# A graph-attention layer on one core: section ends combined in 13 blocks inside the loop, and a final stage whose value bias is added by TensorE

## The chip, the cores and the metric

The kernel runs on one core of a Trainium2 chip. The metric is the device time of one execution in microseconds (us). All times here are in us from the start of the profiled span unless they are marked otherwise. The engines are named as the profile names them: PE (TensorE), DVE (VectorE), ACT (ScalarE), POOL (GpSimd) and SP (SyncE, which here only issues DMAs).

## The reference

400,000 edges, sorted by target, join 12,500 nodes of 128 channels. What must be computed, cut to what matters here:

```python
h = relu(layernorm(x))
msg = (h @ w_src + b_src)[src] + (h @ w_dst)[dst]
msg = msg * edge_weight * radial_mlp(edge_attr)
msg = (msg @ w_sep + b_sep).reshape(E, 8, 32)
score = einsum(smooth_leaky_relu(msg[:, :, :16]), alpha_dot)     # E x 8 heads
att = segment_softmax(score, dst)                                # over each target's edges
out = segment_sum(msg[:, :, 16:] * att, dst)                     # 12500 x 128
return x + out @ w_proj + b_proj
```

## The kernel before

**Node stage** (lines 149 to 347). Two tables `t_src` and `t_dst` are made from x, four tiles of 128 nodes at a time (`quads`, 25 of them), and written to HBM. In passing, `cuts` (line 303, called at quad 20) prepares constants of the edge stage: DVE works out `far` and `tgt`, and PE multiplies the value bias by the projection (`v_out`). `ends_d` holds in HBM the first and the last target of every section.

**Edge loop** (`windows`, line 661). 500 edges make a section, two sections a step. `for k in range(-5, NP)` runs 400 full steps; the order of the instructions on each engine is that of the program text, since `tc.manual_schedule()` is in force. Step k loads, gathers, multiplies and scores the edges of pair k, and sums the weighted values of pair c = k - 13 (`LAG`), because a softmax over 16 sections (one every 8 steps, `MP`) lies between. `gather` (line 742) makes POOL issue an indirect DMA per 128 edges, 3125 in all. `sums` (line 933) adds the values of a section into a window of 64 target rows; ACT copies the sums out of PSUM (`ob`, three buffers). `store_win` writes them to `win`, and `store` writes 63 rows of each window to `agg`, whose address is read from `base`. Two windows can overlap in `agg`, so SP holds a store back until the store before it has landed. `softmax_up`, `softmax_down`, `softmax_exp` and `softmax_T` come at steps with k % 8 = 2, 3, 3 and 4. The PSUM tile `misc` has one buffer, and `mlp1`, `sums`, `softmax_T` and `prep_turn` share it.

**Tail of the loop** (line 1196). 16 more steps (400 to 415) have nothing to gather; they finish the values of the last 13 pairs. Between them stand the `jobs` that combine section ends: a target whose edges cross a section's end has partial sums in several windows, so first and last rows of all 800 sections (1600 ends) are rescaled and added along the list by scans on DVE. The jobs do this in wide pieces: ends, maxima and rows are loaded, then 1536 ends go through `maxima`, `factors`, `columns`, `totals`, `quotients` and `back` at once; the last 64 ends follow after the last step (line 1202). `scatter` (line 1173) writes 13 pieces of 128 combined rows to `agg` by indirect DMAs on POOL.

**Final stage** (line 1251), outside the branch and with a schedule of its own. ACT issues eight loads of x plus bias (`x_fin`, from `xb`); SP loads `agg` in groups of 12 tiles (`load_g`, four buffers). `quotients` (DVE) divides by the softmax sums, `turn` transposes four tiles on PE and copies them on ACT, `finish` multiplies by `w_proj` on PE. On DVE, `finish` then adds the value bias to x once per tile (line 1308) and the product to x once per four tiles (line 1312), and SP stores the result.

Of the kernel before, what the change touches and what calls it, by code (L numbers as in the profile page):

```python
# [30 lines left out]
P = 128  # L31
# [25 lines left out]
def gnn_kernel(ctx: ExitStack, tc: tile.TileContext, a: dict, out: bass.AP):  # L57
# [20 lines left out]
    win = dram.tile([NS * W, ROW], F32, name="win")  # L78
    ends_d = dram.tile([1, 2 * NS + 2], I32, name="ends_d")
# [69 lines left out]
    with tc.tile_pool(name="node", bufs=2) as np_, tc.tile_pool(name="node1", bufs=1) as n1, \  # L149
# [145 lines left out]

        w_score = const.tile([C, C], F32, name="w_score")
# [6 lines left out]
        def cuts():  # L303
# [357 lines left out]
    def windows():  # L661
# [5 lines left out]
        with tc.tile_pool(name="wk2", bufs=2) as sp, tc.tile_pool(name="ps", bufs=1, space=PSUM) as pp, \  # L667
                tc.manual_schedule(), ExitStack() as held:
            lp = held.enter_context(tc.tile_pool(name="ld", bufs=2))
# [277 lines left out]
            def store(c, f):  # L947
                at = nc.sync.value_load(base[0:1, f, c:c + 1])
                nc.sync.dma_start(out=agg[ds(at, W - 1), :], in_=accs[c][f * W:(f + 1) * W - 1, :])


            def load_x(i):
                xs[i] = lp.tile([P, 4, C], F32, name="xs")
# [11 lines left out]

            def has(k):
                return 0 <= k < NP
# [6 lines left out]
            def step(k):  # L974
                c = k - LAG
                if has(c - 2):
                    store_win(c - 2)
                    store(c - 2, 0)
# [11 lines left out]
                if has(c - 2):  # L990
                    store(c - 2, 1)
# [58 lines left out]
                if has(c - 1):  # L1050
                    sums(c - 1)
                if has(k + 1):
# [17 lines left out]
            cp = held.enter_context(tc.tile_pool(name="cm", bufs=1))  # L1070
            NE = 2 * NS
            NA = NE // (4 * P) * 4 * P
            NC = -(-NE // P)
            differ = cp.tile([P, NE + 1], BF16, name="differ")
            cuts = cp.tile([P, NE], BF16, name="cuts")
            mx = cp.tile([P, NE], F32, name="mx")
            up = cp.tile([P, NE + 1], F32, name="up")
            de = cp.tile([P, NE], F32, name="de")
            rn = cp.tile([P, NE], F32, name="rn")
            obs = cp.tile([P, NC, ROW], F32, name="obs")  # L1080
            ids = cp.tile([P, NC], I32, name="ids")
            rows_w = win.rearrange("(s w) c -> s w c", w=W)
            rrs, nodes, tots = {}, {}, {"n": rn}

            def ends_load():
                nodes[0] = cp.tile([P, NE + 2], I32, name="node")
                nc.sync.dma_start(out=nodes[0], in_=ends_d[0:1, :].to_broadcast([P, NE + 2]))
                nodes[1] = cp.tile([NC, 2, P], I32, name="to")
                nc.vector.memset(nodes[1], -1)
                for j in range(2):  # L1090
                    nc.sync.dma_start(out=nodes[1][0:NC - 1, j, :], in_=ends_d[:, 1 + j:1 + j + (NC - 1) * P]
                                      .rearrange("o (g p) -> (o g) p", p=P))
                    nc.sync.dma_start(out=nodes[1][NC - 1:NC, j, 0:NE - (NC - 1) * P],
                                      in_=ends_d[:, 1 + j + (NC - 1) * P:1 + j + NE])

            def maxima_load(e0, e1):
                at = max_d[0:1, e0:e0 + 1]
                nc.sync.dma_start(out=mx[:, e0:e1], in_=bass.AP(
                    at.tensor, at.offset, [[NE, H], [0, C // H], [1, e1 - e0]]))

            def rows_load(g):
                rrs[g] = cp.tile([P, 4, ROW], F32, name="rr", bufs=2)
                q = P // 2
                for i in range(2):
                    nc.sync.dma_start(
                        out=rrs[g][i * q:(i + 1) * q], in_=rows_w[g * 4 * q:(g + 1) * 4 * q, i * (W - 1), :]
                        .rearrange("(j p) c -> p j c", j=4))

            def marks():
                nc.vector.tensor_tensor(differ, nodes[0][:, 1:NE + 2], nodes[0][:, 0:NE + 1], op=ALU.not_equal)  # L1110
                nc.vector.tensor_scalar(cuts, differ[:, 0:NE], RESTART, None, op0=ALU.mult)
                nc.vector.memset(up[:, 0:1], 0.0)
                nc.gpsimd.memset(obs[:, :, C:ROW], 1.0)
                tots["d"] = cp.tile([P, NE], F32, name="node")

            def places():
                on = cp.tile([NC, P], F32, name="on")
                to = nodes[1]
                nc.vector.tensor_tensor(on, to[:, 0, :], to[:, 1, :], op=ALU.is_equal)
                nc.vector.scalar_tensor_tensor(on, on, SKIP, to[:, 0, :], op0=ALU.mult, op1=ALU.add)  # L1120
                pt = pp.tile([P, NC], F32, name="m1")
                nc.tensor.transpose(pt, on, ident[:NC, :NC])
                nc.vector.tensor_copy(ids, pt)

            def maxima(e0, e1):
                nc.vector.tensor_tensor_scan(up[:, 1 + e0:1 + e1], cuts[:, e0:e1], mx[:, e0:e1],
                                             up[:, e0:e0 + 1] if e0 else RESTART, op0=ALU.add, op1=ALU.max)

            def factors(e0, e1):

                e = slice(e0, e1)
                nc.vector.tensor_add(de[:, e], up[:, e0:e1], cuts[:, e])
                nc.vector.tensor_sub(de[:, e], de[:, e], up[:, 1 + e0:1 + e1])
                nc.scalar.activation(de[:, e], de[:, e], AF.Exp)
                nc.vector.tensor_sub(mx[:, e], mx[:, e], up[:, 1 + e0:1 + e1])
                nc.scalar.activation(mx[:, e], mx[:, e], AF.Exp)
                nc.vector.tensor_mul(mx[:, e0 + 1:e1:2], mx[:, e0 + 1:e1:2], differ[:, e0 + 1:e1:2])

            def columns(g):

                pt = pp.tile([P, 2, 4, P], F32, name="p3")
                rx = cp.tile([P, 4, C], F32, name="rx")
                nc.scalar.copy(rx.rearrange("p j (h k) -> p j h k", h=H),
                               rrs[g][:, :, C:ROW].unsqueeze(3).to_broadcast([P, 4, H, C // H]))
                for j in range(4):
                    nc.tensor.transpose(pt[:, 0, j, :], rrs[g][:, j, 0:C], ident)
                    nc.tensor.transpose(pt[:, 1, j, :], rx[:, j, :], ident)
                e = slice(g * 4 * P, (g + 1) * 4 * P)
                for k, r in enumerate(tots.values()):
                    nc.vector.tensor_mul(  # L1150
                        r[:, e].rearrange("p (j s i) -> p j i s", j=4, i=2),
                        pt[:, k].rearrange("p j (i s) -> p j i s", i=2),
                        mx[:, e].rearrange("p (j s i) -> p j i s", j=4, i=2))

            def totals(e0, e1):
                for r in tots.values():
                    nc.vector.tensor_tensor_scan(r[:, e0:e1], de[:, e0:e1], r[:, e0:e1],
                                                 r[:, e0 - 1:e0] if e0 else 0.0, op0=ALU.mult, op1=ALU.add)

            def quotients(e0, e1):  # L1160
                e = slice(e0, e1)
                nc.vector.tensor_scalar(de[:, e], tots["d"][:, e], 1e-16, None, op0=ALU.add)
                nc.vector.reciprocal(de[:, e], de[:, e])
                nc.vector.tensor_mul(mx[:, e], rn[:, e], de[:, e])

            def back(g0, g1):
                pt = pp.tile([P, 4, P], F32, name="pa")
                w = min(P, NE - (g1 - 1) * P)
                for g in range(g0, g1):
                    nc.tensor.transpose(pt[:w, g - g0, :], mx[:, g * P:g * P + w], ident)  # L1170
                nc.scalar.copy(obs[:w, g0:g1, 0:C], pt[:w, 0:g1 - g0, :])

            def scatter(g):
                w = min(P, NE - g * P)
# [189 lines left out]
```

## Time and profile before

| what | us |
|---|---|
| median of 3 runs (lowest, highest) | 4316.28 (4314.72, 4322.2) |
| the profiled execution's own time | 4315.26 |
| its span, first to last instruction | 4313.4 |
| node stage, until the first load of the loop | 0 to 111.2 |
| gathers, first start to last end | 118.4 to 4108 |
| last full step ends on PE | 4115.3 |
| last copy of window sums (L941) ends | 4205.4 |
| first load of `agg` in the final stage (L1268) | 4229.3 |
| end | 4313.4 |

The span is busy on PE for 94%, on DVE for 72%, on POOL for 70% and on ACT for 49%. The windows view puts busy times beside the granted clock of TensorE: 982.8 of 1000 us of PE from 1000 to 2000 at clock 1.00, and 10.4 of 25 us from 4175 to 4200 at clock 0.71. "Idle before" in a row of the timeline is what the engine spent before that instruction, with what ended it. SPq, ACTq and POOLq are the issuing of DMAs.

### The profile page before, as it was taken

The numbers are of one execution on the slowest core, as the hardware profiler recorded it, in microseconds if no ns is written. First come the engines' busy times: TensorE is split into PE (matmuls) and PEld (weight loads), VectorE is DVE, ScalarE is ACT, GpSimd is POOL, SyncE is SP. The second block draws the span as 40 slices with busy tenths as digits, with TensorE's granted clock in tenths as the row PEclk, the third lists the DMA queues.
The fourth block names the chain that finished last, engine by engine and source line by source line (L and its number), as shares of the span: only waits on it lengthen the run. The fifth ranks groups of instructions, "written<-read, shape, count | busy, mean of one in ns | idle before, by whom it ended". The sixth has DMA issues, their size and how long they took to land.

```text
span 4313.4 us, 91919 instructions
## 1 busy us (share of the span) xinstructions
PE 4065.7 (94%) x31567; PEld 2626.4 (61%) x31567; DVE 3101.8 (72%) x5980; ACT 2105.5 (49%) x4995; POOL 3037.4 (70%) x3148
## 2 busy tenths in 40 slices
PE   6679999999999999999999999999999999999974
PEld 5346666666666666666666666666666666666653
DVE  7357777777777777777777777777777777777776
ACT  6335555555455455455555455454555545544521
POOL 0667777777777777777777777777777777777701
PEclk8789999999999999999999999999999999999987
DMA  5667777777777777777777777777777767777725
GB/s 207 196 183 183 183 193 184 192 194 185 194 188 186 192 190 186 192 183 185 198 186 193 185 177 190 183 182 185 175 181 188 177 182 184 182 185 178 173 59 190
DMA packets 598603, 790.10 MB, mean 183 GB/s; under 512 B 125595, under 2 KB 475424, under 8 KB 597996
## 3 DMA queue, kind: packets, MB, share of 16 engines
q1 hardware_dynamic: 394314, 520.94, 43.1%
q0 software_dynamic: 100416, 205.45, 23.2%
q10 hardware_dynamic: 103394, 57.74, 5.1%
q8 instruction: 250, 4.10, 0.4%
q14 instruction: 229, 1.88, 0.1%
HBM read 643.48 MB, written 140.67 MB: 182 GB/s over the span
## 4 chain that ended last, share of the span: by engine, by line
PE 80%; DMA 8%; ACT 3%; DVE 3%; issue 2%; POOL 2%; SPq 1%; ACTq 0%; POOLq 0%; DVEq 0%
PE V L926 16%; PE pa L840 14%; PE misc L937 9%; PE pm L829 6%; PE p L800 6%; PE pm L819 6%; PE p L783 5%; PE m L768 5%; PE m L854 4%; PE pm L822 4%; DMA gs<-t_src,idx 4%; POOL gs L749 2%; PE m L759 2%; ACT L842 1%; DMA agg<-z 1%
## 5 line engine op out<-in xcount | busy, mean ns | idle before, releaser
L749 POOL DMA_INDIRECT gs<-t_src,idx x3125 | 3023.0, 967 | 1082.9 <-issue 778.6
L842 ACT ACTIVATE sl<-pa,c_b_a 128x500 f32<-128x500 f32 x800 | 541.8, 677 | 1004.4 <-PE pa L840 996.8
L926 PEld LDWEIGHTS V<-c_w_v,mT 128*125 128x125 f32 x6192 | 735.3, 188 | 479.8 <-DVE ohT L793 231.9
L928 DVE TENSOR_TENSOR pvx<-V,Pem 125x512 f32<-125x512 f32 x774 | 530.9, 686 | 524.2 <-PE V L926 495.5
L926 PE MATMUL V<-c_w_v,mT 128*125 128x128 f32 x6192 | 875.3, 285 | 0.2 <-DVE pvx L928 0.2
L840 PE MATMUL pa<-mT,c_w_a 128*128 128x500 f32 x1600 | 817.4, 593 | 53.8 <-DVE al L847 51.8
L847 DVE SCALAR_TENSOR_TENSOR al<-pa,sl 128x500 f32<-128x500 f32 x800 | 542.3, 678 | 239.6 <-ACT sl L842 227.0
L822 PEld LDWEIGHTS pm<-ident,gs 128*128 128x128 f32 x2350 | 418.6, 192 | 380.0 <-issue 359.5
L807 DVE SCALAR_TENSOR_TENSOR rad<-p,c_fc_b,w_b 128x500 f32<-128x500 f32 x800 | 553.3, 733 | 104.2 <-PE p L800 101.4
L835 DVE SCALAR_TENSOR_TENSOR mT<-pm,c_b_src,rad 128x500 f32<-128x500 f32 x800 | 553.2, 733 | 79.9 <-PE pm L829 66.1
L937 PE MATMUL misc<-pvx,oh 125*64 125x136 f32 x6400 | 463.7, 288 | 0.0
L937 PEld LDWEIGHTS misc<-pvx,oh 125*64 125x64 f32 x6400 | 361.1, 138 | 163.7 <-ACT eT L761 157.3
L819 PE MATMUL pm<-ident,gs 128*128 128x128 f32 (+9 forms) x2725 | 436.9, 275 | 13.1 <-DMA gs<-t_src,idx 12.7
L800 PE MATMUL p<-h,w3b 64*128 64x500 f32 x1600 | 406.5, 585 | 11.1 <-ACT h L786 11.1
L786 ACT ACTIVATE h<-p,b 128x500 f32<-128x500 f32 x400 | 326.3, 816 | 177.1 <-PE p L783 134.5
L941 ACT COPY ob<-misc 128x136 f32<-128x136 f32 x400 | 108.9, 272 | 618.3 <-PE misc L937 533.7
L822 PE MATMUL pm<-ident,gs 128*128 128x12 f32 (+30 forms) x2350 | 384.2, 244 | 16.5 <-DMA gs<-t_src,idx 15.7
L819 PEld LDWEIGHTS pm<-ident,gs 128*128 128x128 f32 (+9 forms) x2725 | 339.2, 157 | 30.2 <-DMA gs<-t_src,idx 18.3
L829 PE MATMUL pm<-ohT,m 64*128 64x500 bf16 x2400 | 325.6, 378 | 0.0
L840 PEld LDWEIGHTS pa<-mT,c_w_a 128*128 128x128 f32 x1600 | 243.1, 192 | 81.4 <-DVE al L847 65.6
L768 PE MATMUL m<-eT,w1b 64*128 64x250 f32 x800 | 276.7, 426 | 7.5 <-ACT Sp L857 6.5
L768 PE MATMUL misc<-eT,w1b 64*128 64x250 f32 x800 | 276.7, 426 | 0.0
(151 smaller groups left out, 4227.0 us busy)
## 6 DMA issues: line engine op xcount, KB each, us to landing
w_b<-in_edge_weight SPq DMA_DIRECT2D x400, 500.0 KB
d_b<-in_dst SPq DMA_DIRECT2D x400, 250.0 KB
e_t<-in_edge_attr ACTq DMA_DIRECT2D x400, 125.0 KB
gs<-t_src,idx POOLq DMA_INDIRECT x3125
sc_d<-Sp SPq DMA_DIRECT2D x200, 250.0 KB
win<-ob SPq DMA_DIRECT2D x400, 68.0 KB
agg<-ob SPq DMA_DIRECT2D x800, 33.5 KB
md<-t_dst SPq DMA_DIRECT2D x800, 32.0 KB
```

The lines of the kernel that those rows point to most:

```text
L749: nc.gpsimd.indirect_dma_start(out=gs[:, t - t0, :], out_offset=None, in_=t_src[:, :], in_offset=bass.IndirectOffsetOnAxis(ap=idx[:, t:t + ...
L768: nc.tensor.matmul(p1[q], w1b[s, :], eTs[k][s, :], start=True, stop=True)
L800: nc.tensor.matmul(p3s[k][:, f, 0:SEC], w3b[s, :], h2s[k][s, :], start=True, stop=True)
L807: nc.vector.scalar_tensor_tensor(rad[:, s], p3[:, f, 0:SEC], b3, w_g[k][:, s], op0=ALU.add, op1=ALU.mult)
L819: nc.tensor.matmul(pms[k, f][:, a - e0:b - e0], gath[k // 16, t][:n], ident[:n, :n], start=(a == e0), stop=False, is_transpose=True, skip_ ...
L822: nc.tensor.matmul(pms[k, f][:, a - e0:b - e0], gath[k // 16, t], ident[:, a - t * P:n], start=(a == e0), stop=False, skip_group_check=True)
L829: nc.tensor.matmul(pms[k, f], m3[k][s, j, :], ohT[k][s, :], start=False, stop=(j == 2), skip_group_check=True)
L835: nc.vector.scalar_tensor_tensor(mTs[k][:, s], pms.pop((k, f)), b_n, rad[:, s], op0=ALU.add, op1=ALU.mult)
L840: nc.tensor.matmul(pa, w_a, mTs[k][:, f * SEC:(f + 1) * SEC], start=True, stop=True)
L842: nc.scalar.activation(sl, pa, AF.Silu, bias=b_a, scale=1.0)
L926: nc.tensor.matmul(V[:, t, :], mTs[c][:, o:o + T], w_v, start=True, stop=True)
L937: nc.tensor.matmul(acc[f * W:(f + 1) * W, :], ohs[c][:, f * TS + t, :], pvx[c][:, f, t, :], start=(t == 0), stop=(t == TS - 1), skip_group ...
```

## The change

The section ends are no longer combined in wide pieces in the tail. They are cut into 13 blocks of 128 ends (64 sections, 32 steps; the last has 64 ends). Blocks 0 to 10 are combined wholly inside the full steps of the loop, at fixed steps: load at k % 32 = 15, `block_maxima` at 17, `block_factors` at 19, `block_columns` at 20, `block_totals` at 21, `block_out` at 23. Block 11 falls on steps 399 to 407, and block 12 follows the last step. Ends are no longer divided; undivided sums with their weights are kept, and the final stage divides every row. Blocks 0 to 10 are parked in HBM (`obs_d`), and loaded and scattered one per step from step 400 on. `places`, which works out the scatter's row numbers, moves into `cuts` of the node stage. The tail has 14 steps (to 413); in these the window of `sums` is stored in the same step and not two steps later. The last stores and the scatters are declared free of each other.

The final stage moves into the same branch and schedule. Its x is loaded by ACT in the steps from 404 on, one load a step; all groups of `agg` have buffers of their own and are loaded at once; and the value bias is added by TensorE: `turn_has` transposes the 12 columns `has` of a group, and each tile's product gets a second matmul of `hasT` with `vsel`, in which row t of block t holds `v_out`. The pool `ld` moves to the other side of the memory, and `xs` has one buffer instead of two.

```diff
+            places()                        # at the end of cuts(), node stage
-                if has(c - 2):
+                if has(c - 2) and k <= NP:      # so too for store(c - 2, 1)
                     store_win(c - 2)
                     store(c - 2, 0)
...
                 if has(c - 1):
                     sums(c - 1)
+                    if k >= NP:
+                        store_win(c - 1)
+                        store(c - 1, 0)
+                        store(c - 1, 1)
...
+                for j in (k - LATE) // SB, (k - LATE) // SB - 1:     # SB = 32, LATE = 47
+                    o = k - LATE - j * SB
+                    if 0 <= j < NC - 1 and o in stages:
+                        stages[o](j)
...
+            def block_factors(g):
+                w, up, mx = width(g), ups[g], mxs[g][:, 0:width(g)]
+                de = des[g] = sp.tile([P, P], F32, name="de", bufs=1)[:, 0:w]
+                nc.vector.tensor_add(de, up[:, 0:w], cuts.pop(g)[:, 0:w])
+                nc.vector.tensor_sub(de, de, up[:, 1:1 + w])
+                nc.vector.tensor_sub(mx, mx, up[:, 1:1 + w])
+                nc.scalar.activation(de, de, AF.Exp)
+                nc.scalar.activation(mx, mx, AF.Exp)
+                nc.vector.tensor_mul(mx[:, 1:w:2], mx[:, 1:w:2], differ.pop(g)[:, 1:w:2])
+            def block_columns(g):
+                w, rr = width(g), rrs.pop(g)
+                rx = sp.tile([P, C], F32, name="rx", bufs=1)
+                nc.scalar.copy(...)                              # 8 weights spread over 128 columns
+                pt = small()                                     # the PSUM tile misc
+                nc.tensor.transpose(pt[:, 0, 0:w], rr[:w, 0:C], ident[:w, :w])
+                nc.tensor.transpose(pt[:, 1, 0:w], rx[:w, :], ident[:w, :w])
+                ...                                              # two products on DVE
+            def block_rows_out(g, ob):
+                w = width(g)
+                po = small().rearrange("p k q -> p (k q)")
+                nc.tensor.transpose(po[:w, 0:C], tots[g][0][:, 0:w], ident)
+                nc.tensor.matmul(po[:w, C:ROW], tots[g][1][:, 0:w], ident[:, 0:P:P // H], start=True, stop=True)
+                nc.scalar.copy(ob[:w, :], po[:w, 0:ROW])
...
-            for k in range(NP, NP + LAG + 3):
+            for k in range(NP, NP + LAG + 1):
                 step(k)
-                if k - NP in jobs:
-                    jobs[k - NP]()
+                j = k - NP
+                if j < NC - 2:
+                    nc.sync.dma_start(out=combined(j), in_=obs_d[j * P:(j + 1) * P, :])
+                    scatter(j)
+                if j >= 4:
+                    next(x_loads, None)
...
+        def turn_has(i):
+            ph = part_tile()
+            nc.tensor.transpose(ph[:m, 0:P], has.pop(i)[:, 0:m], ident)
+            nc.scalar.copy(hasT[i][:m, :], ph[:m, 0:P])
...
             for t in range(t0, t1):
-                nc.tensor.matmul(py[:n, t - t0, :], qT[:, t - t0, :n], w_proj, start=True, stop=True)
-            for t in range(t0, t1):
-                nc.vector.scalar_tensor_tensor(xt, v_out[:n], has[t0 // XQ][:n, u:u + 1], xt, ...)
+                nc.tensor.matmul(py[:n, t - t0, :], qT[:, t - t0, :n], w_proj, start=True, stop=False)
+                nc.tensor.matmul(py[:n, t - t0, :], hasT[j][:m, :n], vsel[:m, t - starts[j], :],
+                                 start=False, stop=True)
...
         for i in range(Q):
             if i % 3 == 1 and i // 3 + 1 < len(starts):
                 quotients(i // 3 + 1)
+                turn_has(i // 3 + 1)
             if i + 1 < Q:
                 turn(i + 1)
             finish(i)
```

More of the change, by code (lines that the diff above doesn't have):

```diff
@@ L293, in fits, with places @@
                               in_=ends_d[0:1, 1:2 * NS + 1].to_broadcast([P, 2 * NS]))
+        NE = 2 * NS
+        NC = -(-NE // P)
+        ids = const.tile([P, NC], I32, name="ids")
+        def places():
+            to = n1.tile([NC, 2, P], I32, name="to")
+            nc.vector.memset(to, -1)
+            for j in range(2):
+                nc.sync.dma_start(out=to[0:NC - 1, j, :], in_=ends_d[:, 1 + j:1 + j + (NC - 1) * P]
+                                  .rearrange("o (g p) -> (o g) p", p=P))
+                nc.sync.dma_start(out=to[NC - 1:NC, j, 0:NE - (NC - 1) * P],
+                                  in_=ends_d[:, 1 + j + (NC - 1) * P:1 + j + NE])
+            on = n1.tile([NC, P], F32, name="on")
+            nc.vector.tensor_tensor(on, to[:, 0, :], to[:, 1, :], op=ALU.is_equal)
+            nc.vector.scalar_tensor_tensor(on, on, SKIP, to[:, 0, :], op0=ALU.mult, op1=ALU.add)
+            pt = nps.tile([P, NC], F32, name="pb", bufs=1)
+            nc.tensor.transpose(pt, on, ident[:NC, :NC])
+            nc.vector.tensor_copy(ids, pt)
         w_score = const.tile([C, C], F32, name="w_score")
@@ L948, in store @@
                 at = nc.sync.value_load(base[0:1, f, c:c + 1])
-                nc.sync.dma_start(out=agg[ds(at, W - 1), :], in_=accs[c][f * W:(f + 1) * W - 1, :])
+                st = nc.sync.dma_start(out=agg[ds(at, W - 1), :], in_=accs[c][f * W:(f + 1) * W - 1, :])
+                if 2 * c + 1 >= (NC - 1) * (P // 2):
+                    tc.declare_no_dep(st.ins, group="combined", reason="its rows follow those of the blocks")
             def load_x(i):
-                xs[i] = lp.tile([P, 4, C], F32, name="xs")
+                xs[i] = lp.tile([P, 4, C], F32, name="xs", bufs=1)
                 for n, t0, t1 in blocks(*quads[i]):
@@ new lines, in block_out, with scatter @@
+            def block_out(g):
+                if g < NC - 2:
+                    ob = sp.tile([P, ROW], F32, name="obk", bufs=1)
+                    block_rows_out(g, ob)
+                    nc.sync.dma_start(out=obs_d[g * P:(g + 1) * P, :], in_=ob)
+                else:
+                    block_rows_out(g, combined(g))
+                    scatter(g)
+            def scatter(g):
+                w = width(g)
+                st = nc.gpsimd.indirect_dma_start(
+                    out=agg[0:N, :], in_=comb[g][:w, :], in_offset=None,
+                    out_offset=bass.IndirectOffsetOnAxis(ap=ids[:w, g:g + 1], axis=0),
+                    bounds_check=N - 1, oob_is_err=False)
+                tc.declare_no_dep(st.ins, group="combined", reason="each node's row is written once")
+                tc.add_to_no_dep_group("combined", st.ins)
@@ L966, in has, with combined @@
+            comb = {}
+            def combined(g):
+                comb[g] = tail_pool.tile([P, ROW], F32, name="comb", bufs=4)
+                return comb[g]
+            stages = {0: lambda g: (block_load(g), block_rows(g)), 2: block_maxima, 4: block_factors,
+                      5: block_columns, 6: block_totals, 8: block_out}
+            assert NE - (NC - 1) * P == P // 2 and NP - (NC - 1) * SB == SB // 2
             def has(k):
@@ L989, in step @@
                     load_sm((k + 4) // MP)
-                if has(c - 2):
+                if has(c - 2) and k <= NP:
                     store(c - 2, 1)
@@ L1080, in windows @@
[L1080 to L1094, printed above, removed]
@@ L1109, in marks @@
[L1109 to L1123, printed above, removed]
@@ L1139, in columns @@
[L1139 to L1174, printed above, removed]
-                st = nc.gpsimd.indirect_dma_start(
-                    out=agg[0:N, :], in_=obs[:w, g, :], in_offset=None,
-                    out_offset=bass.IndirectOffsetOnAxis(ap=ids[:w, g:g + 1], axis=0),
-                    bounds_check=N - 1, oob_is_err=False)
-                tc.declare_no_dep(st.ins, group="combined", reason="each node's row is written once")
-                tc.add_to_no_dep_group("combined", st.ins)
@@ L1216, in windows @@
-            totals(NA, NE)
-            quotients(NA, NE)
-            back(NC - 1, NC)
-            scatter(NC - 1)
+            tail_pool = held.enter_context(tc.tile_pool(name="fin1", bufs=1, side="right"))
+            x_fin = tail_pool.tile([P, NB, C], F32, name="x_fin")
+            x_loads = load_xb(x_fin)
+            last = NC - 1
+            for k in range(NP, NP + LAG + 1):
+                step(k)
+                j = k - NP
[4 more added lines that the diff above has]
+                    next(x_loads, None)
+                if j == 5:
+                    block_load(last)
+                if j == 6:
+                    block_maxima(last)
+                if j == 7:
+                    block_factors(last)
@@ new lines, in windows @@
+            for _ in x_loads:
+                pass
+            block_rows(last)
+            block_columns(last)
+            block_totals(last)
+            block_rows_out(last, combined(last))
+            scatter(last)
+            work.close()
+            with tc.tile_pool(name="fin", bufs=3) as fp:
+                final(fp, x_fin, lambda i: pp.tile([P, 4, P], F32, name=("pm0", "pm1", "V")[i % 3]),
+                      lambda i: pp.tile([P, 4, C], F32, name=("p3", "pa", "m1")[i % 3]),
+                      lambda: small().rearrange("p k q -> p (k q)"))
@@ new lines, in gnn_kernel @@
+        with tc.tile_pool(name="fin_b", bufs=3) as fp, tc.tile_pool(name="fin1_b", bufs=1) as f1, \
+                tc.tile_pool(name="fin_ps", bufs=2, space=PSUM) as fps, tc.manual_schedule():
+            x_fin = f1.tile([P, NB, C], F32, name="x_fin")
+            for _ in load_xb(x_fin):
+                pass
+            final(fp, x_fin, lambda i: fps.tile([P, 4, P], F32, name="pt"),
+                  lambda i: fps.tile([P, 4, C], F32, name="py"), lambda: fps.tile([XQ, P], F32, name="ph"))
```

260 lines of the change are left out of this document (126 added, 134 removed).

## The prediction

> **What bounds the kernel now.** I read the groups of instructions, then who waits for whom, then the timeline of each stage. They give three regimes.
>
> The edge loop, 118 to 4115, is nine tenths of the time. PE looks like its bound, but this group says otherwise:
>
> ```profile
> L749 POOL DMA_INDIRECT gs<-t_src,idx x3125 | 3023.0, 967 | 1082.9 <-issue 778.6
> ```
>
> A gather takes 0.967 us, and in the timeline each starts 0.30 us after the one before ended. 3125 x 1.272 = 3975 us, of 3990 between the first start and the last end: POOL gathers back to back and is the clock of the loop. PE, 98% busy, follows closely. All its waits for gathers (in total, times, longest), in the view of waits, are:
>
> ```profile
> PE pm L822 <- DMA gs<-t_src,idx: 15.7, 15, 2.2
> PE pm L819 <- DMA gs<-t_src,idx: 12.7, 12, 3.8
> ```
>
> 28.4 us together; the same view for 100 to 300 has 9.5 of them, the start. **PE's slack in the steady loop is thus about 19 us**, and what an edit adds to PE there is free up to that.
>
> The tail, 4115.3 to 4229.3, is 114 us of serial work. From the chain that ended last:
>
> ```profile
> 4129.79 6.48 DMA node<-ends_d
> 4138.90 5.96 DMA agg<-ob
> ...
> 4151.47 4.70 DMA agg<-ob
> ...
> 4184.00 9.76 DVE de L1163
> ...
> 4226.85 2.10 DMA agg<-obs,ids
> ```
>
> A wide load stands ahead of the stores on SP's queue, a store then lands in 5 to 6 us instead of the 1.4 of the quiet tail, and one reciprocal over 1536 columns stops everything for 9.8.
>
> The final stage, 4229.3 to 4313.4, is DVE's (7.6 of every 8 us in the windows from 4253 to 4301). One of its groups of 12 tiles, from the timeline:
>
> ```profile
> 4245.26 0.69 DVE L1312 TENSOR_TENSOR x_fin<-py,x_fin 128x512 f32<-128x512 f32 x1 [4.67 <-PE py L1304]
> ...
> 4245.87 0.20 DVE L1279 TENSOR_SCALAR r<-g 128x96 f32<-128x96 f32 x1
> ...
> 4246.10 0.76 DVE L1280 RECIPROCAL r<-r 128x96 f32<-128x96 f32 x1
> ...
> 4246.89 0.18 DVE L1281 TENSOR_TENSOR has<-r,g 128x12 f32<-128x12 f32 x1
> 4246.99 1.75 DVE L1282 TENSOR_TENSOR q<-g,r 128x1536 f32<-128x1536 f32 x1
> 4248.66 1.13 DVE L1308 SCALAR_TENSOR_TENSOR x_fin<-v_out,has,x_fin 128x128 f32<-128x128 f32 x4
> ...
> 4250.25 0.60 PE L1293 MATMUL pt<-ident,q 128*128 128x128 f32 x4
> 4250.68 1.06 PE L1304 MATMUL py<-c_w_proj,qT 128*128 128x128 f32 x8
> ...
> 4251.58 0.60 PE L1293 MATMUL pt<-ident,q 128*128 128x128 f32 x4
> ```
>
> The group recurs every 8.32 us on DVE (the large products stand at 4246.99, 4255.75, 4264.07 and so on). PE takes 1.33 for 4 transposes and 8 product instructions (4250.25 to 4251.58), 0.111 each.
>
> **The change, part by part**, against this execution (span 4313.4, its own time 4315.26, which is 1.0 below the median).
>
> *Places in the node stage: +6.* DVE sets `to` after `tgt` (ends 100.7), then SP issues four loads (1.3 us in the tail, 4130.2 to 4131.5), the last lands about 2 us later (the small `rb` load, 4209.6 to 4211.8: 2.2), two DVE instructions follow (0.6), then PE transposes. So PE's transpose comes at 105. Behind it on PE stand `turn(22)`, which ran at 98.4, and 9.7 us of matmuls without a gap up to the stage's end; behind DVE's waits stand its copies for them. PE moves by 6.8, less what was cold or waiting. Between +4 and +8; none of it is hidden, for the loop's first load and POOL's first gather wait for the stage's tables.
>
> *Blocks in the loop: 24 us on PE, less the slack of 19: +5.* Eleven blocks. k % 32 = 20 is also the step of `softmax_T`: now PE goes straight on (transposes at 4088.36, next values 4088.90). The two block transposes need `misc`, free when ACT has copied `Pem` (4089.70), and the second needs `rx`, 0.3 later on ACT: values start at about 4090.25, **+1.35**. k % 32 = 19 is the step of `softmax_exp`: two more Exp on ACT (0.3 each by their size against the 0.62 of 500 columns), next to the one that is there, so no further table load; the Silu after them, and with it PE's wait for `al` (0.92 now), comes about 0.5 later: **+0.5**. `block_rows_out`: three PE instructions, **+0.35**. `block_maxima` and `block_totals` (DVE, 1 us each) lie in DVE's idle quarter: step 2 already takes a scan of 1.19 there without a longer step. SP's four loads at k % 32 = 15 (2 us) lie in its waits for `Sp` at odd steps (2.5 us each). 11 x 2.2 = 24. If the slack does not cover it, +24; at 3.5 a block, +38; below nothing is excluded, since the gathers stay as they are.
>
> *The tail: 114 becomes 73: -41.* Steps 400 to 403, the round trip of the last scores through HBM and the last `softmax_T` stay: until about 4141, 26 us. No wide load is left, `misc` and `ob` come free sooner, since each step stores its own window. Nine steps (405 to 413) then go at the pace of SP: two landings, 4204.87 to 4207.76 in the quiet tail, 2.9, with the load of a parked block 3.2: 29 us (PE needs 3.0). After the last sums: stores, load of 64 rows (2.2), transposes to copy (2.9 without the division), one scatter (2.1): 8 us; its twelve predecessors are gone already. Unknown is what x costs in steps 404 to 411: 0.9 MB a step on ACT's queue beside 16 stores. A store lands in 1.43 in the quiet tail and in up to 4.6 in the loop behind loads on its own queue (second store 3969.23, next one released 3973.85). I take 2.1, nearer the quiet row, since x goes on another queue and needs 2.2 of each 3.2 us at the 426 GB/s that 4237 to 4245 shows: +10. Bounds 0 and +51. [...]
>
> *The final stage: +1.* Gone are 3 x 1.13 us of DVE a group, so DVE needs 5. But PE now has 4 transposes and 16 product instructions per four tiles, 20 x 0.111 = 2.22, 6.65 a group, **and a wait**: `turn_has` stands on PE ahead of `turn` and `finish`, and needs `has` of the next group, which on DVE stands behind the add of the quad that PE has just finished. From that add's start to the end of `has` is 1.81 (4245.26 to 4247.07), 1.98 with both signals (0.05 and 0.12). Add the transpose, 0.2: **8.83 us a group against 8.32**. From the first load: 4.2 to land (7.4 now with x beside it; 816 KB at 426 GB/s and 2.2), 10.1 to the second group (first quads at half clock, as at 4239.75 to 4246), 7 x 8.83 = 61.8, last group 5.4, add and store 3.3: 84.8 against 84.1. ACT's wait in issuing x (until 4241.2) goes, and what it held back is held by PE. Between -5 and +6.
>
> Sum: 6 + 5 - 41 + 1 = **-29: 4286 us.**
>
> **Rivals.**
> - *PE pays for every block* (no slack where the stalls fall): -29 + 19 = 4305. For: PE never waits for gathers in long stretches. Against: the waits recur every 300 us or so, and POOL never waits.
> - *Stores slow down under x* to 4.5: 16 x 2.4 = +38, **4324**. For: the 4.70 and 5.96 of the chain. Against: those stood behind loads on their own queue.
> - *The other side: PE at half clock in the final stage.* Now, after idle gaps of 4.1 us and more, four transposes take 0.93 to 1.09 instead of 0.63 and eight product instructions 1.8 to 1.9 instead of 1.06; after gaps up to 2.6 they don't. If the new gaps of 2 us a group tripped it, 25 x 20 x (0.215 - 0.111) = +52: **4338**, slower. It decides from an idle gap somewhere between 2.6 and 4.1. [...]
> - *The wait of `turn_has` is hidden* and only PE's 6.85 a group counts: 8 x 2 = -16, 4270. Against: the order of both queues.
>
> **Numbers.** Forecast 0.62 (4270 to 4300), blocks paid 0.13, slow stores 0.10, half clock 0.07, hidden wait 0.08. The range, 4262 to 4320, reaches over the bounds of node stage, stores and loop. A measurement of this kernel tells about 0.2% from no change, 8.6 us, so the line is 4307.7: faster 0.76 (forecast, hidden, most of blocks paid), same 0.14, slower 0.10.
>
> **What would show it.** Right: POOL's gathers still 0.30 apart, and PE's waits for them nearly gone; first gather at 124; first load of `agg` 73 us after the last full step and not 114; PE's rows of `has` 8.8 apart, each after an idle gap of 2 on DVE's `has`. Wrong: L749 waiting for PE, stores over 3 us apart while x loads, groups of 6.9 or of 14 us. The forecast fails most easily in the landing of the stores, and in how evenly PE's slack is spread.

## The result, and the profile after

The changed kernel takes **4416.46 us** (median of 4 runs, 4414.62 to 4425.62) where the kernel before takes 4315.65 (4 runs on the same chip): ratio **1.0234**, interval 1.0217 to 1.0252. It is 101 us slower; the forecast was 4286. In the runs from before_again on, told below, the edge loop of every kernel took over a third longer than here (the kernel before 5770 and 5800 us), so of those mainly tail and final stage are read.

The profiled executions differ by 101.0 us (4313.4 to 4414.4). I divide both at the same marks: POOL's first gather, the start of the last full step's sums, the first load of `agg`, the end. (The tail is counted from the start of those sums here, 1.15 us more than in the prediction.)

| stage | before | after | difference | forecast |
|---|---|---|---|---|
| to the first gather | 118.4 | 124.1 | +5.7 | +6 |
| loop | 3995.7 | 4010.8 | +15.1 | +5 |
| tail | 115.1 | 89.4 | -25.7 | -41 |
| final stage | 84.1 | 190.1 | **+105.9** | +1 |

So the loss is the final stage. The loop's lines are as foreseen: the gathers have kept their pace, and PE's waits for them (view of waits: total, times, longest) have shrunk from 28.4 us to 9.0.

```profile
L772 POOL DMA_INDIRECT gs<-t_src,idx x3125 | 3025.7, 968 | 1092.0 <-issue 775.6 <-DMA sm<-same 121.9 <-DMA gs<-t_src,idx 54.0
```

```profile
PE pm L842 <- DMA gs<-t_src,idx: 8.2, 6, 3.5
...
PE pm L845 <- DMA gs<-t_src,idx: 0.8, 1, 0.8
```

The final stage was DVE's and is now PE's. From the timeline of the changed kernel, PE over one quad:

```profile
4284.85 0.38 PE L1288 MATMUL misc<-ident,has 128*12 128x128 f32 x1 [1.90 <-DVE has L1279]
4285.02 1.06 PE L1298 MATMUL V<-ident,q 128*128 128x128 f32 x4
4285.88 0.64 PE L1311 MATMUL pa<-c_w_proj,qT 128*128 128x128 f32 x2
4286.44 0.79 PE L1312 MATMUL pa<-vsel,hasT 12*128 12x128 f32 x2
4287.16 0.80 PE L1311 MATMUL pa<-c_w_proj,qT 128*128 128x128 f32 x2
4287.89 0.79 PE L1312 MATMUL pa<-vsel,hasT 12*128 12x128 f32 x2
...
4291.50 1.11 PE L1298 MATMUL pm<-ident,q 128*128 128x128 f32 x4
```

The wait for `has`, 1.90 us, is the forecast one (1.98). But a product of two instructions starts every 0.72 us where the forecast had 0.22. DVE's adds show what a quad costs, 6.53 us apart, with DVE idle in between:

```profile
4269.92 0.69 DVE L1316 TENSOR_TENSOR x_fin<-pa,x_fin 128x512 f32<-128x512 f32 x1 [5.15 <-PE pa L1312]
4276.45 0.69 DVE L1316 TENSOR_TENSOR x_fin<-m,x_fin 128x512 f32<-128x512 f32 x1 [5.84 <-PE m L1312]
4282.98 0.69 DVE L1316 TENSOR_TENSOR x_fin<-p,x_fin 128x512 f32<-128x512 f32 x1 [5.84 <-PE p L1312]
```

And the windows of the same stage have the granted clock at half (PEclk, first number behind the busy times) although PE is busy nine tenths of the time:

```profile
core 0: us, PE busy (x) PEld busy (x) DVE busy (x) ACT busy (x) POOL busy (x), PEclk, DMA share, GB/s
4250.00:4300.00 50.00, 46.20 (x144) 33.52 (x143) 10.28 (x15) 4.61 (x9) 0.00 (x0) 0.50 0.10 38
4300.00:4350.00 50.00, 44.29 (x137) 31.77 (x137) 11.45 (x19) 4.02 (x8) 0.00 (x0) 0.50 0.10 38
```

Three theories: **T1**, matmuls whose number of weight rows differs from that of their neighbour are dear; **T2**, accumulating, or changing weights each time, is dear; **T3**, the clock is low for a reason of its own (few rows at work, or the wait for `has`).

### The profile page after: what moved, and what is told of

Its sections match the earlier page's. It is cut to its first block, busy times and chain, and to the rows that moved or that the text cites. A ratio compares the mean times of both kernels' runs of the same rounds, so it can differ in the third digit from the quotient of the medians.

```text
span 4414.4 us, 92479 instructions
## 1 busy us (share of the span) xinstructions
PE 4176.4 (95%) x31798; PEld 2695.6 (61%) x31798; DVE 3073.4 (70%) x6009; ACT 2109.6 (48%) x5043; POOL 3041.7 (69%) x3147
## 5 line engine op out<-in xcount | busy, mean ns | idle before, releaser
L772 POOL DMA_INDIRECT gs<-t_src,idx x3125 | 3025.7, 968 | 1092.0 <-issue 775.6
## 6 DMA issues: line engine op xcount, KB each, us to landing
agg<-ob SPq DMA_DIRECT2D x800, 33.5 KB
```

What stands on the lines that cost most here:

```text
L772: nc.gpsimd.indirect_dma_start(out=gs[:, t - t0, :], out_offset=None, in_=t_src[:, :], in_offset=bass.IndirectOffsetOnAxis(ap=idx[:, t:t + ...
```

## The experiments

### The final stage

**dve_bias**: the bias back on VectorE.

```diff
-                nc.tensor.matmul(py[:n, t - t0, :], hasT[j][:m, :n], vsel[:m, t - starts[j], :], ...)
+                nc.vector.scalar_tensor_tensor(xt, v_out[:n], has[j][:n, u:u + 1], xt, ...)
```

> The changed kernel with one part undone: the value bias is added by VectorE again, one instruction per tile, and the 12-row matmuls, their transposes and the selector tile are gone. All theories put the +106 us of the final stage into that part, so the final stage (first load of agg to the end) should fall from 190.1 us to some 80 to 85 us and the whole to about 4306 to 4313 us. If the final stage stays above 120 us, the loss lies in something else there (the loads of agg, PSUM buffers shared with the loop) and all theories about the matmuls fall.

Measured: final stage 82.5 us; 4288.96 against 4305.71 of the kernel before on the same chip, ratio 0.9957 (0.9941 to 0.9974). The whole loss lies in this part, and the rest of the change is a gain.

**k128** and **k32**: the same instructions, flags and selector padded with zeros.

```diff
-            has[i] = fp.tile([P, XQ], F32, name="has")
+            has[i] = fp.tile([P, 128], F32, name="has")   # k32: 32
+            nc.vector.memset(has[i], 0.0)
-            m = min(XQ, NB - starts[i])
+            m = 128
```

> The changed kernel with the counted flags held in a tile of 128 columns (zeros from 12 on), so that the bias matmuls have 128 rows like the others; their number, order and accumulation are unchanged. T1 (the alternation of 12-row and 128-row weights costs the time): PE falls back to 0.11 to 0.24 us per instruction, the final stage to 80 to 100 us, the whole to 4305 to 4328 us. T2 (accumulating into the same place, or changing weights at every matmul, costs it, whatever the rows): the final stage stays at about 190 us, the whole at about 4416 us. T3 (TensorE's clock is low because few rows work): near T1's time, with the granted clock back above 0.9.

> The changed kernel with the flags padded to 32 rows rather than 128. T1 with a price for any change of row count: stays at about 190 us in the final stage, as with 12 rows. T3 (clock by working rows): little change as well, 12 to 32 rows of 128. If only a row count that is no multiple of 32 is dear, the final stage falls to 80 to 100 us.

Measured: k128 98.3 us, 4301.58 against 4305.71, ratio 0.9988 (0.9979 to 0.9998); k32 190.2 us, 4388.56 in one run. T2 falls: k128 has the same accumulation and the same changes of weights. 32 rows are as dear as 12 (190.2 and 190.1 us).

**grouped**: a quad's four projections first, then its four bias matmuls, 2 changes of row count in place of 8. (In this order it leaves out part of the result, relative error 0.23; instructions and shapes are those of the changed kernel.)

```diff
             for t in range(t0, t1):
                 n = rows(t)
                 nc.tensor.matmul(py[:n, t - t0, :], qT[:, t - t0, :n], w_proj, start=True, stop=False, ...)
+            for t in range(t0, t1):
+                n = rows(t)
                 nc.tensor.matmul(py[:n, t - t0, :], hasT[j][:m, :n], vsel[:m, t - starts[j], :], ...)
```

> The changed kernel with the 12-row matmuls kept, but the four projections of a quad first and then its four bias matmuls: 2 changes of row count per quad in place of 8. T1 (a price per change of row count): the excess of 4.3 us per quad falls to about a quarter, 3.3 us per quad, the final stage to about 110 us. T2 (a price per accumulating matmul) and T3 (a low clock because few rows work): no fall, 6.5 us per quad and about 190 us.

Measured: 119.2 us, 4328.77 in one run, so T1 holds. Its timeline at full clock:

```profile
4245.31 1.06 PE L1311 MATMUL pa<-c_w_proj,qT 128*128 128x128 f32 x8
4246.30 1.15 PE L1315 MATMUL pa<-vsel,hasT 12*128 12x128 f32 x8
4247.38 0.66 PE L1298 MATMUL pm<-ident,q 128*128 128x128 f32 x4
```

Eight instructions take 0.99 and 1.08 us here, against 0.89 in k128 (four products 0.223 apart): a change of row count costs 0.10 to 0.19 us here at full clock. The windows of this stage show that the clock does rise here, and falls again:

```profile
4223.70:4253.70 30.00, 25.07 (x174) 22.38 (x173) 12.12 (x20) 5.20 (x10) 0.00 (x0) 0.90 0.27 103
4253.70:4283.70 30.00, 25.41 (x129) 23.00 (x130) 11.09 (x17) 4.28 (x9) 0.00 (x0) 0.66 0.16 62
```

So few rows at work are not by themselves what holds the clock at half: grouped has as many products of 12 rows as the changed kernel. Of T3 the wait for `has` remains.

What holds the clock down stayed open, for k128 has dips of its own. Its timeline behind a wait for `has`:

```profile
4245.74 0.33 PE L1287 MATMUL misc<-ident,has 128*128 128x128 f32 x1 [1.99 <-DVE has L1278]
...
4246.35 0.39 PE L1310 MATMUL pa<-c_w_proj,qT 128*128 128x128 f32 x2
...
4247.62 0.64 PE L1310 MATMUL pa<-c_w_proj,qT 128*128 128x128 f32 x2
...
4250.65 0.39 PE L1310 MATMUL m<-c_w_proj,qT 128*128 128x128 f32 x2
```

Products go from 0.22 to 0.43 apart some 1 us after the wait and stay so for 3.4 us (4246.8 to 4250.2); then all is full speed until the next wait. Six of the eight waits of 1.99 to 2.08 us are followed by such a dip, which begins 0.2 to 1.1 us behind the wait; behind those that end at 4236.76 and 4277.61 the products stay 0.22 apart. In the kernel before, three gaps of 2.49 to 2.62 us (they end at 4265.89, 4282.52 and 4299.15) went without one. So half clock followed a gap of some 2 us six times of eight, and gaps of some 2.5 us not at all: here its length alone does not decide it. Is such a gap what holds the clock down in the changed kernel?

**nogap12** and **nogap128**: the quotients of the next group one quad earlier, so that PE need not wait; with 12 rows and with 128.

```diff
-            if i % 3 == 1 and i // 3 + 1 < len(starts):
+            if i % 3 == 0 and i // 3 + 1 < len(starts):
                 quotients(i // 3 + 1)
+            if i % 3 == 1 and i // 3 + 1 < len(starts):
                 turn_has(i // 3 + 1)
```

> The changed kernel with its 12-row matmuls as they are, but the quotients of the next group issued one quad earlier, so that the flags are there when TensorE turns them and its wait of 1.90 us per group is gone. Theory that the wait is what holds the clock down (as k128 shows dips to half clock after that wait): the clock rises to 0.9 or more and the alternation costs half, so the final stage falls from 190 us to some 100 to 110 us. Theory that the alternation itself holds it down (the array stands still while each 128-row and 12-row weight is loaded): the clock stays at 0.50, only the eight waits go, and the final stage falls to 173 to 176 us.

> The same shift of the quotients with the flags padded to 128 rows. If each group of k128 paid 1.99 us of waiting and, after it, 3.4 us at half clock (1.7 us lost), the eight later groups give back 8 x 3.7 = 30 us: final stage 98.3 to about 68 us, the whole some 4270 us against 4302 for k128. Rival: only the waits go, or VectorE and the stores of the output take over: final stage 80 to 85 us, the whole about 4285 us.

Measured: nogap12 173.8 us (4376.89, one run); nogap128 **71.2** us, 4272.74 against 4309.52, ratio 0.9922 (0.9906 to 0.9939). Windows of nogap12, then of nogap128:

```profile
4220.00:4250.00 30.00, 30.00 (x94) 21.92 (x95) 6.35 (x11) 2.60 (x5) 0.00 (x0) 0.50 0.09 36
4250.00:4300.00 50.00, 50.00 (x156) 36.27 (x155) 12.82 (x18) 5.45 (x11) 0.00 (x0) 0.50 0.11 43
```

```profile
4214.30:4230.00 15.70, 15.70 (x144) 15.70 (x143) 10.33 (x19) 4.55 (x10) 0.00 (x0) 1.00 0.50 178
4230.00:4250.00 20.00, 20.00 (x182) 20.00 (x182) 14.03 (x24) 5.80 (x12) 0.00 (x0) 1.00 0.31 119
```

Both keep PE busy without a gap; one has half the clock and a third of the instructions per us. The difference is the row count alone. So in k128 the wait costs what it idles and, six times of eight, a dip behind it; in nogap12, with row counts that alternate at every product, the clock stands at 0.50 in every window from 4201 to the end. PEld differs too: with 128 rows weight loads run all the time (20.00 of 20.00 us in nogap128), each starting 0.11 us ahead of its product (4213.81 and 4213.92) beside the one before; with 12 rows they run 73% of the time (36.27 of 50.00 us in nogap12), and in the changed kernel a load starts at the mark of its own product (both 4286.44). Whether that is what keeps the clock at half is not shown.

**nogap64**: nogap128 with 64 rows.

> Nogap128 with the flags padded to 64 rows rather than 128. If any change of row count between neighbouring matmuls is dear, the final stage stays at some 174 us at half clock as in nogap12; if only 32 rows or fewer are dear, it is at 71 us as in nogap128.

Measured: 174.2 us in the final stage, as with 12. A window of it:

```profile
5780.00:5830.00 50.00, 50.00 (x155) 36.31 (x156) 13.44 (x23) 4.65 (x10) 0.00 (x0) 0.50 0.10 37
```

So 12, 32 and 64 rows next to 128 are all dear: 173.8 and 190.1, 190.2, and 174.2 us, against 71.2 and 98.3 with 128 rows.

### The tail

**late_max**: nogap128 with the last block's maxima and factors in steps 10 and 11, not 6 and 7. In the changed kernel VectorE stands still there:

```profile
4183.31 0.23 DVE L1021 TENSOR_TENSOR differ<-node 128x64 bf16<-128x64 int32 x1 [10.96 <-DMA node<-ends_d]
```

```diff
-                if j == 6:
+                if j == 10:
                     block_maxima(last)
-                if j == 7:
+                if j == 11:
                     block_factors(last)
```

> Nogap128 with the maxima and factors of the last block issued in steps 10 and 11 of the last steps rather than 6 and 7. Theory: the changed kernel's tail is long because VectorE stands 10.96 us for the last block's node numbers, whose load is queued on SP behind the stores of agg (3.8 to 4.8 us per pair there), with the last steps' values behind it: end of the last full step to the first load of agg falls from 85 to 88 us to some 74 to 77 us, the whole 9 to 11 us below nogap128. Rival: SP's slow store pairs bound the tail anyway, and the stall only takes their place: less than 3 us gained.

Measured: tail 83.9 us, 4274.15 against 4309.52; nogap128 beside it 85.7 and 4272.74, and k128 and nogap12, also without this edit, 85.1 and 85.5. My theory falls: the stall (10.96 us in the changed kernel, 7.70 in nogap128) is gone, but that gave at most 2 us, so something else, the rival says SP, is late as well.

**x_final** and **x_final_late**: the loads of x behind the last scatter; the second with late_max's edit too.

```diff
-                if j >= 4:
-                    next(x_loads, None)
...
             scatter(last)
+            for _ in x_loads:
+                pass
```

> Nogap128 with the loads of x moved out of the last steps to behind the last scatter, as late as in the kernel before. Theory: in the tail SP is the bound (it issues the stores of agg in pairs, the second behind the first's landing), and the loads of x lengthen a pair from 1.8 to 3.8 to 4.9 us, four times in nogap128; without them the end of the last full step to the first load of agg falls from 85.7 to some 75 to 77 us, while the final stage pays at most 17 us for the same bytes beside the loads of agg. Rival: the pairs are slow for another reason (the scatters of the combined rows), and the tail stays at 84 to 86 us.

> X_final with the last block's maxima and factors in steps 10 and 11 as in late_max. If SP's stores bound the tail with the x loads gone too, it is as x_final within 2 us; if VectorE's stall is what is late next, another 3 to 8 us go.

Measured: tail 80.4 and 79.4 us, final stage 75.1 and 76.0. SP's store pairs, in nogap128 beside a load of x, and in x_final:

```profile
4155.86 4.94 SPq L972 DMA_DIRECT2D agg<-ob  x2
...
4167.39 4.61 SPq L972 DMA_DIRECT2D agg<-ob  x2
```

```profile
5671.45 1.90 SPq L972 DMA_DIRECT2D agg<-ob  x2
...
5675.00 1.94 SPq L972 DMA_DIRECT2D agg<-ob  x2
```

The loads of x do lengthen the pairs and cost the tail 5 us, but the final stage pays 4 back. They are not the only cause of a slow pair: x_final's first one behind the round trip still takes 3.51 us (5659.99). The whole: 5781.18 and 5791.89 against 5769.65 of the kernel before, ratios 1.0030 (1.0002 to 1.0058) and 1.0032 (1.0003 to 1.0062), with the longer loop named above.

### The loop

**no_blocks**: nogap128 without blocks 0 to 10; the tail scatters rows of `win` in their place.

```diff
-                    if 0 <= j < NC - 1 and o in stages:
+                    if NC - 2 <= j < NC - 1 and o in stages:
-                    nc.sync.dma_start(out=combined(j), in_=obs_d[j * P:(j + 1) * P, :])
+                    nc.sync.dma_start(out=combined(j), in_=win[j * P:(j + 1) * P, :])
```

> Nogap128 with the blocks 0 to 10 left out of the loop (their rows are not combined; the tail scatters rows of win in their place, and the last two blocks start afresh). The sums of the last full step then come earlier by what the eleven blocks cost the loop, which the run of the same call without this edit shows: 5 us by the forecast, about 15 us by the difference of the two first traces, up to 38 us if TensorE pays for every instruction.

Measured: loop 3993.2 us, nogap128 and late_max beside it 3988.2 and 3991.0 with the blocks; the whole 4277.18 in one run. All seven traces from dve_bias to late_max have this loop with its blocks and took 3987.8 to 3992.7. So with the blocks in, the loop differs by up to 23 us between traces, and the 15.1 us of the first pair don't come with the blocks alone. One wait sets the first trace apart (view of waits from 200 to 4000; the changed kernel, then nogap128):

```profile
PE misc L921 <- ACT ob L964: 14.3, 17, 1.6
```

```profile
PE misc L921 <- ACT ob L964: 0.2, 1, 0.2
```

`softmax_T` waits for ACT to free `misc`: 14.3 us in 17 waits here, at most 1.2 us in each of the seven others, with the same code of the loop. But that wait can account for little of the length, because POOL sets the pace. The group of the gathers, in nogap128 and then in no_blocks:

```profile
L772 POOL DMA_INDIRECT gs<-t_src,idx x3125 | 3008.1, 963 | 1087.3 <-issue 760.0
```

```profile
L772 POOL DMA_INDIRECT gs<-t_src,idx x3125 | 3024.7, 968 | 1085.5 <-issue 755.9
```

A gather takes 968 ns in the changed kernel's first trace (3025.7 us in all, shown above) and in no_blocks, 967 in the kernel before, 963 to 965 in the seven. That is up to 18 us over 3125 gathers. From the first gather's start to the last one's end the first trace takes 3995.8 us and nogap128 3973.2: this is all by which their loops differ. From there to the last full step's sums, which is how far PE trails POOL at the end, both take 15.0 us. So the whole loop of no_blocks can't be set against that of nogap128, since its gathers were slower. What can be compared is how far PE trails: 6.1 and 5.2 us in the two traces without blocks (the kernel before, no_blocks), 8.6 to 15.0 in the eight with them. That is 3 to 10 us more, with the forecast's +5 among them. The +15.1 of the first pair are 8.9 us of trailing and 6.2 between first and last gather. Why gathers take 963 ns in one trace and 968 in another stays open.

**before_again**, and, on one chip, **before_pair**, **after_pair**, **no_blocks_pair** and **x_final_pair**: the same kernels again, for traces side by side.

> The kernel before, unchanged, for a trace beside the others of this call. The first pair of traces put the sums of the last full step 20.8 us later in the changed kernel, 5.7 us of it in the node stage, 15.1 us in the loop; no_blocks says that the blocks cost the loop nothing that one pair of traces shows (its last full step ended 4.9 us after that of nogap128). If the 15 us belong to the change, they stand here against x_final and x_final_late as well; if they are how far two executions of the loop differ, the distance is 6 to 12 us, places included.

> The kernel before, unchanged: its trace is the base for the loop in the three other runs of this call. Its last full step's sums are expected 3990 to 3996 us after POOL's first gather, as in the first trace (4114.14 - 118.41 = 3995.7).

> The changed kernel, unchanged. From POOL's first gather to the last full step's sums it took 4010.8 us in its first trace (4134.92 - 124.08), 15.1 more than before. If the blocks cost that, it is 15 more than before_pair here too; by the forecast of this step it is 5 more; whole time some 100 us above before either way.

> Nogap128 with the blocks 0 to 10 left out of the loop, as in no_blocks: their rows are not combined. What it takes from the first gather to the last full step's sums, against after_pair, is the price of the blocks alone; against before_pair, that of the rest of the change in the loop. Theory of the forecast: 5 below after_pair and level with before_pair. Rival (the blocks are free, and the 15 us came from something else in the loop or from two executions that differ): level with after_pair.

> X_final, in executions beside before_pair. Its tail was 80.4 us and its final stage 75.1, against 85.7 and 71.2 of nogap128, so the whole should be 1 to 2 us below nogap128's, some 35 to 38 us below the kernel before, unless the loop differs.

With the longer loop POOL's idle time was 2515 to 2700 us, against 1083 to 1092 in the other traces, so the gathers no longer stand back to back and the forecast's premise for the loop does not hold. The loop took 5425 us in before_again, 5506 and 5510 in x_final and x_final_late beside it; on the chip of the pairs 5469 in before_pair, 5493 in no_blocks_pair and 5572 in after_pair. So after_pair is 103 us above before_pair and 79 above no_blocks_pair, where the forecast would have 5 and 5. But these are single traces, and the whole time of the kernel before alone ranged from 5752 to 5839 us on that chip, so the price of the blocks there is not shown. Tail and final stage come out again as in the table: 113.5 and 84.1 (before_again), 115.6 and 84.3 (before_pair), 91.5 and 190.1 (after_pair), 88.1 and 71.4 (no_blocks_pair), 81.0 and 75.1 (x_final_pair). Whole times: 5741.97, 5788.74, 5980.30, 5779.04 in single runs, and x_final_pair 5836.06, ratio 1.0042 (0.9998 to 1.0087).

## Why the prediction was wrong

- **The failed step** is *The final stage: +1*, in its words "4 transposes and 16 product instructions per four tiles, 20 x 0.111 = 2.22". The 0.111 was taken from matmuls of 128 rows among their like. With 128 rows the step is right: nogap128's quads start 2.24 us apart (4211.02, 4213.26). With 12 rows next to 128 a quad takes 6.53. At the half clock of k128's dips 20 instructions make 20 x 0.213 = 4.3, and eight changes of row count add 8 x (0.72 - 0.43) = 2.3: 6.6. So of the extra 4.3 us about half is the clock and half the changes. The step bounded its sum by -5 and +6, though no row that it read mixes row counts. Why the clock stays at half while they alternate is open. (The large products of DVE stand at 4255.67 and 4263.99, not at 4255.75 and 4264.07; the period of 8.32 holds from there on.)
- **The rival "PE at half clock"** had the right place and sign, with half the price (+52) and another trigger. It set the deciding gap between 2.6 and 4.1 us; in k128 six of eight gaps of 1.99 to 2.08 us were followed by half clock, and in nogap12 it stays at half (0.50) without a gap. Nor do all rows that it read agree: behind the gap of 4.14 us that ends at 4290.84 the four transposes still took 0.63 us, and only the product instructions behind them were longer, 1.77.
- **The wait of `turn_has`** was right, 1.90 us against 1.98, and so was its place. In k128 the two groups without a dip recur in 8.98 and 9.08 us, where the forecast had 8.83. Removed together with the half-clock dips (k128 to nogap128) the wait gave back 27.1 us, not the 16 of the rival "hidden": eight waits of 2 us and six dips of 1.7.
- **The tail, -41**: -25.7. What was mis-sized is the pace of SP, not x. Without x (x_final) the parts are 27.4 us to the first sums after the round trip (forecast 26, which is 27 from the mark used here), 41.3 to the end of the last store pair (29) and 11.8 to the first load (8). There are ten store pairs where the forecast had nine steps. With a block's load they recur at 3.4 to 3.6 us, not 3.2, and three of the first four intervals are 5.1 to 6.0: the slow first pair, the loads of the last block (2.1 us), and a wait of SP for ACT (1.8). x costs 5 (85.7 to 80.4) to 9 us (89.4 to 80.4), forecast 10.
- **The loop, +5**: +15.1 in the first pair of traces, and the medians of that pair leave 15 for it too; less in the runs measured next. For instance nogap128's median is 36.8 below the kernel before, of which places (+6.0), tail (-29.4) and final stage (-12.9) make -36.3 and leave the loop nothing; the same sum leaves 6 in dve_bias. (Tail and final stage of the kernel before are those of its first trace.) The mechanism, gathers at their pace and PE trailing by a few us more, agrees with 3 to 10 us of trailing; the forecast's size holds only within what such sums can tell, and not where the loop was a third longer. The blocks' Exp brought no further table load, as foreseen: there are 50 at the softmax's Exp and 49 at the Silu behind it, 1.28 us each, before and after.
- **The places, +6**: 5.7.

With the one term mended (nogap128) the change does what was forecast for it, and a bit more: 4272.74, 0.78% under the kernel before on its chip. There that version beats both kernels; with the longer loop it was not timed, and x_final, timed only there, was 0.3% slower than the kernel before although its tail and final stage were 42 us shorter: the loop took that back.

## What to carry to other kernels

A matmul moved to an engine with idle time is not priced by the count of its instructions: look at what stands before and after it. Here a product of two instructions took 0.72 us instead of 0.22 with 12 rows of weights next to 128, at a granted clock of 0.50 (the changed kernel); padding with zeros to the neighbours' row count brought the final stage from 173.8 to 71.2 us (nogap12 and nogap128). And where a stage shares a queue, the longest stall of the tail (10.96 us of VectorE) may hide behind a queue that is late anyway: without the stall the tail fell by at most 2 us here (late_max), so move it alone before you count on it.

## What the runs showed of the hardware that was not expected

- Between neighbouring f32 matmuls of 128 columns, a change between 128 and 12 rows of weights cost 0.10 to 0.19 us at full clock (grouped) and, by an estimate from the 0.72 us per product of the changed kernel and the 0.43 of k128's dips, about 0.29 at half, when it came at every product. 32 and 64 rows gave the same final stage as 12 (190.2 and 190.1, 174.2 and 173.8 us). 128 padded rows cost 0.11 per instruction (nogap128).
- The granted clock stayed at 0.50 through 130 us with PE busy all the time, 50.00 of 50 us (nogap12), while row counts alternated at every product; with two changes in a quad it reached 0.90 over 30 us (grouped).
- Six of eight gaps of 1.99 to 2.08 us on PE were followed by 3.4 us at half clock, starting 0.2 to 1.1 us after work resumed (k128); the same work without the gaps ran at 1.00 (nogap128). Three gaps of 2.49 to 2.62 us in the kernel before were followed by full speed.
- Two stores of 33.5 KB on one queue took 1.8 to 2.0 us without loads of x (once 3.5; the ten pairs of x_final's last steps) and, in four pairs of nogap128, 3.8 to 4.9 beside loads of 0.9 MB on another queue.
